# A selective-scan stage laid out with states on partitions, its input replicated by DMA, and the next batch prepared beside it

## The chip, the cores and the metric

The kernel runs on one core of one Trainium2 chip. The metric is the device time of an execution in microseconds; the comparison uses the median of several runs. A core has five engines with instruction queues of their own: TensorE (PE in the profile; PEld are its weight loads), VectorE (DVE), ScalarE (ACT), GpSimd (POOL) and SyncE (SP), which here issues most of the DMA transfers. Each queue is worked off in order.

## The reference

A block of four layers on x of 4 batches x 512 tokens x 512 channels, each added to x after a layernorm of it:

1. a gated MLP with int8-style smoothing and rounding (`smooth_quant`);
2. a feed-forward layer of inner width 1376 whose weights are looked up in a table of 16 values (`lut_weights`, `lut_ffn`);
3. a selective scan (a state-space layer) on the context input, gated by x;
4. a mixture of 32 experts with the 8 best for each token.

The change is about the third. Cut to what matters, for each batch, with 512 inner channels d, 16 states n and 512 time steps l:

```python
x = einsum('bld,ed->bel', hidden_states, in_proj_w)
x = silu(causal_conv4(x) + conv_b)                  # u
dt_low, Bm, Cm = split(einsum('bdl,ed->bel', x, x_proj_w))
dt = softplus(dt_proj_w @ dt_low + dt_proj_b)
A = -exp(A_log)
# over l, for every d and n:
state = state * exp(dt * A) + (dt * u) * B
y = sum_n state * C
y = (y + D * u) * silu(z)                           # z = layernorm(x)
```

## The kernel before, in words

The work is written as Python generators. A `yield` marks a step, `weave` takes steps from several generators in proportion to the step counts it is given, and a planner then orders the instructions by priority with costs of its own, within what data and buffers allow. The order of each engine's queue is therefore set when the kernel is built. `keep_in_program_order` fixes single DMAs in that order; `issue_after` (in the change) queues instructions directly behind a given one.

The stages are:

- **Smooth-quant and lookup** (L187 to L342). Four batches of `smooth_quant` are woven with the lookup of the feed-forward weights: one-hot rows on VectorE (L326) and matmuls with 32 weight columns on TensorE (L332). SP loads the index rows (L319), which GpSimd's own DMAs have laid out (L303).
- **Scan stage** (L988 to L1005). `lut_ffn` runs as one stream over all batches. A step (L366 to L381) has 16 matmuls of 256 columns, a tanh on ScalarE and two VectorE instructions. Woven with it, for each batch b, are `scan(b)`, and from b = 1 on `gate(b-1)` ahead of them and `route(b-1)` among them.
- **Experts** (L1006 to L1030): gathers (L811) and scatter-adds (L879) by indirect DMA on GpSimd, matmuls on TensorE. The first eight experts run beside the gate and the routing of the last batch. Then the two sums are added to x (L904 to L919).

`scan(b)` first prepares the batch. It loads the context cT (L428), and for each of four blocks of 128 channels it makes the projection pi (L433), its copy xin, the convolution (L440, L444) and u (L447, L448). Then it projects to dt, B and C (px, L454), and stores B and C in DRAM (xdbl, L457). The softplus follows (L465 to L476): Abs, Exp and Ln on ScalarE, the maximum (L470), a correction "lost" for small values (L472, L473) and two adds on VectorE. dt*u is one GpSimd product of 2048 columns (L477). The buffers u, dt, dtu and sz exist once, so a batch can't be prepared while the one before it is still scanned or gated.

Then come 64 units, each of one block e of channels and one state n. The 128 partitions are channels. For each n and each pair of blocks, `bc` brings one row of B and one of C to all partitions (L487: 512 KB, three buffers). A unit is: exp(dt*A) into a PSUM bank st (ScalarE, L490), dBu = dtu*B (GpSimd, L492), the scan along time (VectorE, L493), sc = st*C (VectorE, L495), and a matmul by the identity that adds sc into py[e] (TensorE, L496). An fp32 matmul appears as two records. After 16 states, L499 adds D*u.

`gate` multiplies by silu of the layernorm of x, transposes, and adds to x. `route` normalizes x, stores it to DRAM (L598, L599), makes the router's logits, the eight best, and 32 indirect scatters per batch into tables (L707). `layernorm` has two small VectorE instructions around a power on GpSimd (L102 to L105). `routing_constants` clears 16 tables and the two sums in DRAM from a zero tile (L580, L582), on SP's queue at the beginning of the scan stage.

Of the kernel before, what the change touches and what calls it, by code (L numbers as in the profile page):

```python
# [38 lines left out]
NST = 16  # L39
RANK = 16  # L40
# [18 lines left out]
class Kernel:  # L59
# [33 lines left out]
    def layernorm(self, dst, src, n):  # L93
# [8 lines left out]
        nc.vector.tensor_scalar(rs, mv[:, :, 1], LN_EPS, None, ALU.add)  # L102
        nc.gpsimd.tensor_tensor(rs, rs, self.mhalf[:, :n], ALU.pow)
        off = self.small.tile([P, n], F32, tag="ln_off", name="ln_off")
        nc.vector.scalar_tensor_tensor(off, mv[:, :, 0], -1.0, rs, ALU.mult, ALU.mult)  # L105
# [238 lines left out]
    def lut_ffn(self, bp, b):  # L344
# [4 lines left out]
        for hb in range(TPB // 2):  # L349
            xb = self.x[:, b * TPB + 2 * hb : b * TPB + 2 * hb + 2, :]  # L350
            xn = bp.tile([P, 2, HID], F32, tag="xn", name="xn", bufs=1)
            self.layernorm(xn, xb, 2)
            xT = bp.tile([P, KH, W], F32, tag="xT", name="xT", bufs=1)
            for k in range(0, KH, 2):
                pt = self.bank("t", "pt_x")
                for kk in range(2):
                    for i in range(2):
                        nc.tensor.transpose(
                            pt[:, kk * W + i * P : kk * W + (i + 1) * P],
                            xn[:, i, (k + kk) * P : (k + kk + 1) * P],  # L360
                            self.ident,
                        )
                nc.scalar.copy(xT[:, k : k + 2, :], pt.rearrange("p (k w) -> p k w", k=2))
# [35 lines left out]
    def scan_weights(self, mp):  # L399
# [15 lines left out]
        self.A = mp.tile([P, KH, NST], F32, name="A", bufs=1)  # L415
        nc.sync.dma_start(out=self.A, in_=t["A_log"])
        nc.scalar.activation(self.A, self.A, AF.Exp)
        nc.vector.tensor_scalar(self.A, self.A, -1.0, None, ALU.mult)
# [3 lines left out]
    def scan(self, mp, b):  # L422
# [3 lines left out]
        conv_b, dt_b, skip = (self.vecs[:, i, :] for i in range(3))  # L426
        cT = mp.tile([P, DC // P, S], F32, tag="sz", name="cT", bufs=1)
        nc.sync.dma_start(out=cT, in_=t["ctxT"][b].rearrange("(k p) l -> p k l", p=P))  # L428
        u = mp.tile([P, KH, S], F32, tag="u", name="u", bufs=1)
        for e in range(KH):  # L430
            pi = self.bank("d", "pi")
# [4 lines left out]
            xin = mp.tile([P, S + 3], F32, tag="dBu", name="xin", bufs=3)  # L436
            nc.gpsimd.memset(xin[:, :3], 0.0)
            nc.scalar.copy(xin[:, 3:], pi)
            acc = mp.tile([P, S], F32, tag="sc", name="acc", bufs=3)
# [3 lines left out]
            for j in (2, 1, 0):  # L443
                nc.vector.scalar_tensor_tensor(  # L444
                    acc, xin[:, j : j + S], self.conv_w[:, e, j : j + 1], acc, ALU.mult, ALU.add
                )
# [78 lines left out]
    def routing_constants(self, rp):  # L525
# [47 lines left out]
        for seen in self.seen:  # L573
            nc.vector.memset(seen, 0.0)
# [511 lines left out]
```

## Time and profile before

| | us |
|---|---|
| median of the three runs | 2109.53 (2107.18 to 2111.25) |
| profiled execution, its own time | 2106.76 |
| its span, first to last instruction | 2105.0 |
| smooth-quant and lookup | 0 to 322 |
| scan stage, to the end of its last scans | 322 to 1244 |
| experts | 1244 to 2063 |
| last sum | 2063 to 2105 |

Over the whole span TensorE is busy for 1825.7 us (87%), VectorE for 1240.6 (59%), GpSimd for 970.8 (46%) and ScalarE for 661.5 (31%). The mean granted clock of TensorE is 0.935. The numbers of one profiled execution are compared with one another; they differ from the median of the runs by some 3 us.

How to read the lines in this document: a line of a *group* gives the source line, engine, operation, output<-inputs, shapes and count, then the busy time in us and the mean length of one in ns, then how long the engine stood idle just before such instructions, and what ended those waits. A line of a *stretch* gives the window, its length, and the busy time of each engine in it (with instruction counts), the granted clock of TensorE, the share of the DMA engines that was busy, and GB/s. A line *in order of time* gives the start, the length, the engine and the instruction.

### The profile page before, as it was taken

Reading aid. Unit: us, or ns where it says so; the run is one execution under the profiler, and the core shown is the slowest. Engines: PE = TensorE matmul, PEld = TensorE weight load, DVE = VectorE, ACT = ScalarE, POOL = GpSimd, SP = SyncE. Lnnn points to the kernel's source line nnn. Section 1 sums busy time; section 2 is a strip of 40 time slices with the busy share of each in tenths; the row PEclk is TensorE's granted clock in tenths of the full one; section 3 lists DMA queues with packets and bytes.
Section 4 is the critical chain, followed back from the end, with each engine's and each line's share of the span. In section 5 each row is a group of like instructions: output and inputs, shape, how many; then the busy total and the mean of one; then the engine's idle time right before and its main releaser. Section 6 shows DMA issues by size and latency. Waiting matters only on the chain. (4 is left out here: it accounts for less than half of the span.)

```text
span 2105.0 us, 23555 instructions
## 1 busy us (share of the span) xinstructions
PE 1825.7 (87%) x8367; PEld 1072.7 (51%) x8377; DVE 1240.6 (59%) x2061; ACT 661.5 (31%) x1267; POOL 970.8 (46%) x836
## 2 busy tenths in 40 slices
PE   4777859988988998898979978859999999999980
PEld 2443427543554655464645535445656556656540
DVE  6788753599989878996799864213222223323232
ACT  1553451433433325332423232202222222222210
POOL 3111011166328742775158765655655555555531
PEclk9899979999989999899889989969999999999995
DMA  9421106144325422453225485657978887777655
GB/s 263 113 99 55 71 8 227 32 121 129 111 52 116 108 76 79 102 112 79 82 49 119 104 223 143 138 125 171 193 175 192 176 185 164 165 184 158 149 130 178
DMA packets 187699, 271.30 MB, mean 129 GB/s; under 512 B 43778, under 2 KB 90338, under 8 KB 187572
## 3 DMA queue, kind: packets, MB, share of 16 engines
q1 hardware_dynamic: 145828, 185.36, 31.3%
q0 software_dynamic: 41744, 84.34, 21.1%
q8 instruction: 68, 1.11, 0.2%
q14 instruction: 59, 0.48, 0.1%
HBM read 208.92 MB, written 69.18 MB: 132 GB/s over the span
## 5 line engine op out<-in xcount | busy, mean ns | idle before, releaser
L836 PE MATMUL pg<-exT,egu 128*128 128x320 f32 (+1 forms) x1536 | 404.4, 421 | 8.6 <-DVE eh L853 3.7
L492 POOL TENSOR_TENSOR dBu<-dtu,bc 128x512 f32<-128x512 f32 x256 | 322.6, 1274 | 149.5 <-DMA bc<-xdbl 108.8
L879 POOL DMA_INDIRECT sums<-ey,to x168 | 262.2, 1561 | 269.3 <-DMA sums<-ey,to 129.2
L836 PEld LDWEIGHTS pg<-exT,egu 128*128 128x128 f32 x1536 | 290.8, 192 | 127.5 <-issue 38.7
L493 DVE TENSOR_TENSOR_SCAN st<-st,dBu 128x512 f32<-128x512 f32 x256 | 308.0, 1221 | 57.9 <-ACT st L490 28.5
L496 PE MATMUL py<-sc,ident 128*128 128x512 f32 x512 | 267.1, 637 | 46.0 <-DVE sc L495 42.7
L490 ACT ACTIVATE st<-dt,A 128x512 f32<-128x512 f32 x256 | 170.7, 686 | 388.7 <-DVE sc L495 366.5
L811 POOL DMA_INDIRECT xg<-xln,tokens x168 | 163.6, 974 | 103.5 <-PE pt_g L824 40.8
L332 PE MATMUL pw<-oh,lut_t 128*32 128x344 bf16 (+1 forms) x2052 | 131.5, 376 | 70.7 <-DVE oh L326 70.7
L853 DVE SCALAR_TENSOR_TENSOR eh<-eh,pg 128x320 f32<-128x320 f32 (+5 forms) x144 | 61.1, 424 | 215.1 <-ACT eh L852 120.4
L371 PE MATMUL pgu<-xT,wg 128*128 128x256 f32 (+1 forms) x704 | 184.3, 400 | 1.3 <-DVE o L238 0.4
L865 PE MATMUL po_e<-ed,eh 128*128 128x512 f32 (+1 forms) x336 | 171.9, 631 | 11.3 <-ACT ey L878 3.9
L371 PE MATMUL pgu<-xT,wu 128*128 128x256 f32 (+1 forms) x704 | 179.8, 395 | 0.0
L496 PEld LDWEIGHTS py<-sc,ident 128*128 128x128 f32 x512 | 93.5, 197 | 162.0 <-DVE sc L495 106.6
L876 DVE TENSOR_SCALAR ey<-po_e,gates 128x512 f32<-128x512 f32 x64 | 45.8, 747 | 212.7 <-PE po_e L869 119.8
L495 DVE TENSOR_TENSOR sc<-st,bc 128x512 f32<-128x512 f32 x256 | 167.6, 679 | 5.2 <-PE py L496 0.5
L371 PEld LDWEIGHTS pgu<-xT,wg 128*128 128x128 f32 (+1 forms) x704 | 135.4, 197 | 60.7 <-issue 40.2
L387 PE MATMUL po_f<-wd,h 128*128 128x512 f32 (+1 forms) x352 | 164.3, 604 | 0.0
L878 ACT ACTIVATE ey<-po_e,gates 128x512 f32<-128x512 f32 (+1 forms) x104 | 68.8, 684 | 284.4 <-PE po_e L869 143.1
L371 PEld LDWEIGHTS pgu<-xT,wu 128*128 128x128 f32 (+1 forms) x704 | 138.2, 198 | 33.5 <-issue 12.3
L707 POOL DMA_INDIRECT table<-i_tok,to x128 | 127.1, 993 | 34.7 <-issue 23.2
L332 PEld LDWEIGHTS <-lut_t 128*32 128x32 bf16 x2052 | 59.8, 106 | 124.2 <-issue 84.4
(254 smaller groups left out, 2061.7 us busy)
## 6 DMA issues: line engine op xcount, KB each, us to landing
bc<-xdbl SPq DMA_DIRECT2D x128, 512.0 KB
egu<-in_w_gate SPq DMA_DIRECT2D x40, 384.0 KB
ix<-idx_b SPq DMA_DIRECT2D x16, 688.0 KB
egu<-in_w_up SPq DMA_DIRECT2D x40, 256.0 KB
ed<-in_w_down SPq DMA_DIRECT2D x40, 256.0 KB
ed<-in_w_down SPq DMA_DIRECT2D x80, 128.0 KB
sums<-zero SPq DMA_DIRECT2D x2, 4608.0 KB
acc<-sums SPq DMA_DIRECT2D x16, 512.0 KB
```

The costliest lines, as they stand in the source:

```text
L332: nc.tensor.matmul(pt[i][32 * c : 32 * c + 32, :step], lhsT=self.lut_t[:, j, g, :], rhs=oh[:, c * n + i * step : c * n + (i + 1) * step], ...
L371: nc.tensor.matmul(pg[:m, j * W : (j + 1) * W], lhsT=w[:, k, c * P : c * P + m], rhs=xT[:, k, :], start=k == 0, stop=k == KH - 1,)
L387: nc.tensor.matmul(po, lhsT=h[:m, c, i * P : (i + 1) * P], rhs=self.wd[:m, c, :], start=c == 0, stop=c == NIC - 1,)
L490: nc.scalar.activation(st, dt[:, e, :], AF.Exp, scale=self.A[:, e, n : n + 1])
L492: nc.gpsimd.tensor_tensor(dBu, dtu[:, e, :], bc[:, 0, :], ALU.mult)
L493: nc.vector.tensor_tensor_scan(st, st, dBu, 0.0, ALU.mult, ALU.add)
L495: nc.vector.tensor_tensor(sc, st, bc[:, 1, :], ALU.mult)
L496: nc.tensor.matmul(py[e], lhsT=self.ident, rhs=sc, start=n == 0, stop=n == NST - 1)
L811: nc.gpsimd.indirect_dma_start(out=xg[:m, :], out_offset=None, in_=xln, in_offset=bass.IndirectOffsetOnAxis(ap=tokens[:m, lo + j, col : co ...
L836: nc.tensor.matmul(pg[i][:, :hs], lhsT=w[:, k, i * P : (i + 1) * P], rhs=xT[:, k, z : z + hs], start=k == 0, stop=k == KH - 1,)
L865: nc.tensor.matmul(po[j][:m, :], lhsT=h[:, 0, b : b + m], rhs=wd[:, 0, :], start=True, stop=False)
L879: nc.gpsimd.indirect_dma_start(out=sums[j], out_offset=bass.IndirectOffsetOnAxis(ap=to[:m, lo + j, col : col + 1], axis=0), in_=y[:m, :], ...
```

## The change

- `scan(b)` is split into `prepare(b)` and `scan(b)`. `prepare(0)` is woven with six feed-forward steps; `prepare(b+1)` is a stream beside `scan(b)`. u has two buffers. The banks of PSUM are divided anew (t=2, m=2, y=1, d=3 for t=2, m=2, y=2, d=2).
- `prepare` computes the convolution from PSUM directly, with no copy xin. Softplus is done in blocks of 512 columns: the maximum becomes a Relu on ScalarE, and three of the VectorE instructions become GpSimd ones. dt and dt*u of each block go to DRAM (`dts`), by a DMA that GpSimd issues.
- A unit of the scan now has 16 states x 8 channels on the 128 partitions. Its dt and dt*u come by one DMA that replicates 8 rows 16 times (`d`: 512 KB a unit, four buffers); B and C for the whole batch stay in one tile BC. Of each four units, one has its product with C on GpSimd. Four units at a time are summed over states by four matmuls with 32 weight columns each, into the four quarters of py.
- `layernorm`'s two small VectorE instructions go to GpSimd; the feed-forward and the gate normalize one block at a time.
- `route` takes its weights from a mask instead of a product of one-hot rows, and the one-hot rows become bf16.
- The zeros for tables and sums (`scratch`) are written in the lookup stage, in 28 steps.

The diff, cut to its core:

```diff
     def layernorm(self, dst, src, n):
...
-        nc.vector.tensor_scalar(rs, mv[:, :, 1], LN_EPS, None, ALU.add)
+        nc.gpsimd.tensor_scalar(rs, mv[:, :, 1], LN_EPS, None, ALU.add)
         nc.gpsimd.tensor_tensor(rs, rs, self.mhalf[:, :n], ALU.pow)
...
-        nc.vector.scalar_tensor_tensor(off, mv[:, :, 0], -1.0, rs, ALU.mult, ALU.mult)
+        for i in range(n):
+            nc.gpsimd.tensor_scalar(off[:, i : i + 1], mv[:, i, 0:1], rs[:, i : i + 1], -1.0, ALU.mult, ALU.mult)
...
+    def prepare(self, mp, b):
...
+        u = self.u[b] = mp.tile([P, KH, S], F32, tag="u", name="u", bufs=2)
         for e in range(KH):
...
-            xin = mp.tile([P, S + 3], F32, tag="dBu", name="xin", bufs=3)
-            nc.gpsimd.memset(xin[:, :3], 0.0)
-            nc.scalar.copy(xin[:, 3:], pi)
-            acc = mp.tile([P, S], F32, tag="sc", name="acc", bufs=3)
+            acc = mp.tile([P, S], F32, tag="sc", name="acc", bufs=6)
...
             for j in (2, 1, 0):
+                a = 3 - j
                 nc.vector.scalar_tensor_tensor(
-                    acc, xin[:, j : j + S], self.conv_w[:, e, j : j + 1], acc, ALU.mult, ALU.add
+                    acc[:, a:], pi[:, : S - a], self.conv_w[:, e, j : j + 1], acc[:, a:], ALU.mult, ALU.add
                 )
...
-        nc.sync.dma_start(out=self.xdbl[b].rearrange("g n l -> (g n) l"), in_=xd)
+        nc.scalar.dma_start(out=self.xdbl[b].rearrange("g n l -> (g n) l"), in_=xd)
...
-            nc.scalar.activation(dtu[:, e, :], pd, AF.Abs, bias=dt_b[:, e : e + 1])
-            nc.vector.tensor_scalar(dt[:, e, :], pd, dt_b[:, e : e + 1], 0.0, ALU.add, ALU.max)
-        nc.scalar.activation(dtu, dtu, AF.Exp, scale=-1.0)
-        nc.vector.tensor_scalar(lost, dtu, 1.0, -1.0, ALU.add, ALU.add)
-        nc.vector.tensor_tensor(lost, dtu, lost, ALU.subtract)
-        nc.scalar.activation(dtu, dtu, AF.Ln, bias=1.0)
-        nc.vector.tensor_tensor(dtu, dtu, lost, ALU.add)
-        nc.vector.tensor_tensor(dt, dt, dtu, ALU.add)
-        nc.gpsimd.tensor_tensor(dtu, dt, u, ALU.mult)
+            d = mp.tile([P, 2, S], F32, tag="dt", name="dt", bufs=2)
+            dt, w = d[:, 0, :], d[:, 1, :]
+            nc.scalar.activation(w, pd, AF.Abs, bias=dt_b[:, e : e + 1])
+            nc.scalar.activation(dt, pd, AF.Relu, bias=dt_b[:, e : e + 1])
+            nc.scalar.activation(w, w, AF.Exp, scale=-1.0)
+            lost = mp.tile([P, S], F32, tag="sc", name="lost", bufs=6)
+            nc.vector.tensor_scalar(lost, w, 1.0, -1.0, ALU.add, ALU.add)
+            nc.gpsimd.tensor_tensor(lost, w, lost, ALU.subtract)
+            nc.scalar.activation(w, w, AF.Ln, bias=1.0)
+            nc.gpsimd.tensor_tensor(dt, dt, lost, ALU.add)
+            nc.gpsimd.tensor_tensor(dt, dt, w, ALU.add)
+            nc.gpsimd.tensor_tensor(w, dt, u[:, e, :], ALU.mult)
+            nc.gpsimd.dma_start(out=self.dts[b, e * P : (e + 1) * P], in_=d)
+            yield
+
+    def scan(self, mp, b):
...
+        BC = mp.tile([P, 2, S], F32, tag="BC", name="BC", bufs=1)
+        for g in range(2):
+            nc.sync.dma_start(
+                out=BC[:, g, :], in_=self.xdbl[b, 1 + g].unsqueeze(1).to_broadcast([NST, CPT, S])
+            )
+        for e in range(KH):
+            py = self.bank("y", f"py{e}")
+            for v in range(4):
+                scs = []
+                for j in range(4):
+                    r0 = e * P + 32 * j + CPT * v
+                    d = mp.tile([P, 2, S], F32, tag="d", name="d", bufs=4)
+                    nc.sync.dma_start(
+                        out=d, in_=self.dts[b, r0 : r0 + CPT].unsqueeze(0).to_broadcast([NST, CPT, 2, S])
+                    )
                     st = self.bank("d", "st")
-                    nc.scalar.activation(st, dt[:, e, :], AF.Exp, scale=self.A[:, e, n : n + 1])
+                    i = (e * 4 + v) * 4 + j
+                    nc.scalar.activation(st, d[:, 0, :], AF.Exp, scale=self.A[:, i : i + 1])
                     dBu = mp.tile([P, S], F32, tag="dBu", name="dBu", bufs=3)
-                    nc.gpsimd.tensor_tensor(dBu, dtu[:, e, :], bc[:, 0, :], ALU.mult)
-                    nc.vector.tensor_tensor_scan(st, st, dBu, 0.0, ALU.mult, ALU.add)
-                    sc = mp.tile([P, S], F32, tag="sc", name="sc", bufs=3)
-                    nc.vector.tensor_tensor(sc, st, bc[:, 1, :], ALU.mult)
-                    nc.tensor.matmul(py[e], lhsT=self.ident, rhs=sc, start=n == 0, stop=n == NST - 1)
+                    nc.gpsimd.tensor_tensor(dBu, d[:, 1, :], BC[:, 0, :], ALU.mult)
+                    sc = mp.tile([P, S], F32, tag="sc", name="sc", bufs=6)
+                    if j == 0:
+                        nc.vector.tensor_tensor_scan(sc, st, dBu, 0.0, ALU.mult, ALU.add)
+                        nc.gpsimd.tensor_tensor(sc, sc, BC[:, 1, :], ALU.mult)
+                    else:
+                        nc.vector.tensor_tensor_scan(st, st, dBu, 0.0, ALU.mult, ALU.add)
+                        nc.vector.tensor_tensor(sc, st, BC[:, 1, :], ALU.mult)
+                    scs.append(sc)
...
+                with ExitStack() as behind:
+                    for j in (3, 0, 1, 2):
+                        y = nc.tensor.matmul(
+                            py[32 * j : 32 * j + 32, :],
+                            lhsT=self.sum_states[:, v, :],
+                            rhs=scs[j],
+                            start=v == 0,
+                            stop=v == 3,
+                        )
+                        if j == 3:
+                            behind.enter_context(self.tc.issue_after(y.ins))
...
     def gate(self, mp, b):
...
         for e in range(KH):
+            sz = mp.tile([P, 1, S], F32, tag="sc", name="sz", bufs=6)
+            self.layernorm(sz, xb[:, e : e + 1, :], 1)
+            th = mp.tile([P, 1, S], F32, tag="sc", name="th", bufs=6)
...
     def clear(self, zero, tables, n):
...
         for s in self.sums:
+            for a in range(0, NT + 2, 3):
+                z = nc.sync.dma_start(
+                    out=s.rearrange("(a p) d -> p a d", p=P)[:, a : a + 3, :],
+                    in_=zero[:, :HID].unsqueeze(1).to_broadcast([P, 3, HID]),
+                )
+                self.tc.keep_in_program_order(z)
+                yield
...
     def route(self, rp, b):
...
-        ow = tl([P, TPB * TOPK, NE], F32, "ow")
-        nc.vector.tensor_tensor(
-            ow, oh, top.rearrange("p i k -> p (i k)").unsqueeze(2).to_broadcast([P, TPB * TOPK, NE]), ALU.mult
-        )
-        nc.vector.tensor_reduce(w, ow.rearrange("p (i k) e -> p i e k", i=TPB), AX.X, ALU.add)
+        mask = self.mask(rp, oh)
+        nc.vector.tensor_tensor(w, pr, mask, ALU.mult)
+        nc.vector.tensor_tensor(w, w, m.unsqueeze(2).to_broadcast([P, TPB, NE]), ALU.mult)
...
+                weave((islice(sq, 40), 40), (islice(lookups, 36), 36))
+                weave((sq, 30 * NB - 40), (lookups, 4 * len(k.jobs) - 36), (k.scratch(lc), 4 * CHAINS))
+            k.banks(early, t=2, m=2, y=1, d=3)
...
+            weave((k.prepare(mp, 0), preps), (islice(ffn_, 6), 6))
             k.routing_constants(rp)
...
             for b in range(NB):
-                n = steps + (4 if b == 0 else 0)
+                n = steps - (2 if b == 0 else 0)
                 streams = [(k.scan(mp, b), units), (islice(ffn_, n), n)]
+                if b + 1 < NB:
+                    streams.append((k.prepare(mp, b + 1), preps))
```

`sum_states`, which is new, holds ones where a partition's channel is that of the column, so that a matmul by it adds the 16 states of 8 channels. `A` is spread to the same layout by a small matmul at the start.

## The prediction

> **What bounds the kernel now.** I read the stretches first. They split the 2105.0 us span into smooth-quant and lookup (0 to 322 us), the scan stage (322 to 1244), experts, and a last sum. The change is almost wholly in the second, so I cut that at its scans (420 to 557, 645 to 780, 830 to 1000, 1070 to 1213) and at the gaps between, in which one batch is gated and the next prepared.
>
> ```profile
> core 0: us, PE busy (x) PEld busy (x) DVE busy (x) ACT busy (x) POOL busy (x), PEclk, DMA share, GB/s
> 322.00:420.00 98.00, 96.51 (x344) 64.48 (x344) 41.75 (x92) 29.55 (x47) 8.58 (x14) 0.97 0.40 139
> 420.00:557.00 137.00, 120.69 (x333) 58.38 (x334) 130.76 (x163) 51.64 (x79) 81.15 (x68) 0.98 0.41 111
> 557.00:645.00 88.00, 76.42 (x264) 44.78 (x263) 76.87 (x134) 34.55 (x56) 27.91 (x24) 0.90 0.30 87
> ...
> sum 922.00, PE 841.07 PEld 492.79 DVE 753.60 ACT 326.33 POOL 473.48; mean PE 93.45 PEld 54.75 DVE 83.73 ACT 36.26 POOL 52.61
> ```
>
> In a scan VectorE is full (130.76 of 137); before the first scan it has 41.75 of 98, and in a gap GpSimd stands still. No engine is full over the whole stage: VectorE's 753.6 of 922 is what a better overlap could squeeze. The groups name the work, and the instructions in order of time give the real pitch, since VectorE instructions overlap in the record.
>
> ```profile
> L492 POOL TENSOR_TENSOR dBu<-dtu,bc 128x512 f32<-128x512 f32 x256 | 322.6, 1274 | 149.5 <-DMA bc<-xdbl 108.8 <-DVE st L493 23.6 <-DVE x L394 5.6
> L493 DVE TENSOR_TENSOR_SCAN st<-st,dBu 128x512 f32<-128x512 f32 x256 | 308.0, 1221 | 57.9 <-ACT st L490 28.5 <-POOL dBu L492 26.7 <-issue 0.8
> L496 PE MATMUL py<-sc,ident 128*128 128x512 f32 x512 | 267.1, 637 | 46.0 <-DVE sc L495 42.7
> L490 ACT ACTIVATE st<-dt,A 128x512 f32<-128x512 f32 x256 | 170.7, 686 | 388.7 <-DVE sc L495 366.5
> L495 DVE TENSOR_TENSOR sc<-st,bc 128x512 f32<-128x512 f32 x256 | 167.6, 679 | 5.2 <-PE py L496 0.5
> ```
> ```profile
> 440.06 0.68 DVE L495 TENSOR_TENSOR sc<-st,bc 128x512 f32<-128x512 f32 x1
> 440.66 1.22 DVE L493 TENSOR_TENSOR_SCAN st<-st,dBu 128x512 f32<-128x512 f32 x1
> 441.79 0.41 DVE L381 SCALAR_TENSOR_TENSOR h<-g,pgu 128x256 f32<-128x256 f32 x1
> ```
>
> Pitch: product 0.60 us (440.66 - 440.06), scan 1.13. ScalarE waits 366.5 us for L495, so it is early. Two more views price what is new.
>
> ```profile
> 59.52 2.74 PE L332 MATMUL pw<-oh,lut_t 128*32 128x344 bf16 x49
> ```
> ```profile
> 610.66 4.50 POOL L477 TENSOR_TENSOR dtu<-dt,u 128x2048 f32<-128x2048 f32 x1 [29.45 <-DVE seen L684]
> ```
> ```profile
> 610.84 4.36 DVE L692 TENSOR_SCALAR over<-chosen 128x32 f32<-128x32 f32 x1
> 615.12 0.41 DVE L380 SCALAR_TENSOR_TENSOR g<-g,pgu 128x256 f32<-128x256 f32 x1
> 615.45 1.09 DVE L684 TENSOR_TENSOR seen<-seen,mask 128x32 bf16<-128x32 bf16 x1
> ```
>
> The first: 49 matmuls on 32 columns in 2.74 us, 56 ns each, though one alone is recorded at about 319 ns: column groups run side by side. The others: a tiny VectorE instruction lasts as long as the GpSimd product beside it.
>
> **What the Trainium skill says.** SBUF — State Buffer, section "Who interferes with whom": a VectorE instruction with two SBUF inputs, or in a two-port mode, and a GpSimd instruction that reads SBUF shut each other out for a whole instruction. L692 and L684 agree; the scan and C's product, with one operand in PSUM, keep their length beside GpSimd, as it also says. TensorEngine Tiling (Array Packing), "Key Properties": column tiles run independently, but a change of tiling mode drains the engine. The 56 ns agree with the first; no row isolates a drain. GPSIMD Engine Reference, "Performance versus the Vector engine": an add of 2048 takes 4497 ns on GpSimd against 2293 on VectorE; L477's 4505 and L476's 2291 agree, so work moved to GpSimd costs twice. DMA: Bandwidth & Descriptors, "Why a DMA increments its semaphore by 16 and not by 1": the engines used follow from both patterns' outer sizes; here 16 copies and 128 partitions, so all 16 (no run shows it yet).
>
> **Part by part, within the 922 us.**
>
> VectorE. A quarter of C's products leaves: 64 x 0.60 = -38.4. Softplus: 16 maxima to ScalarE at 0.67, -10.7; 12 instructions of 2048 columns (L473, L475, L476; pitch 2.2) to GpSimd, -26.4; L472 in quarters, 16 x 0.35 for 4 x 1.13, +1.1. Norm arithmetic: -5. The routing masks save some 2.6 per batch, three in the stage, -7.8. Sum: 753.6 - 87.2 = 666. Scans stay 256 x 1.13. Against that, with GpSimd nearly always busy, some 80 instructions that need the shared port (per batch 4 "lost", 4 u, 8 of the gate, a few of routing) wait. Bounds: none to a whole product, 0 to 100 us; I take half a product, 0.6 x 80 = 48. **714.**
>
> GpSimd. 473.5, plus 64 C products x 1.25 (pairs take 2.50) = 80; softplus 64 x 1.25 less L477's 18 = +62; 16 stores of dt and dt*u at 1.1 (L303's issues took that), +18; norms, two small instructions each for about 44 at 0.1 to 0.3 (a memset of three columns 0.10, iota 0.16), taken 0.2, and 16 more powers at 0.55, +27; the 0.30 gaps that L707's 96 scatters show, +29. **690.** Every product, store and norm is in one queue with dBu: what waits there holds up the next scan.
>
> TensorE, by pitch. A feed-forward half-matmul of 256 columns takes 0.216 us (8 in 1.73), one of 512 takes 0.43 (38 in 16.5). Feed-forward: 1408 x 0.216 + 352 x 0.43 + transposes 8 = 463; projections 128 x 0.43 = 55; gate and router (L518, L602, L607) about 33; scan 512 x 0.43 = 220: 771. The change still makes 256 scan matmuls, of 32 columns each, in 64 groups of four. Each is two records. Fully side by side a group takes 2 x 0.43 = 0.86, one after another 3.44; if both halves of a matmul must follow each other in the queue while the next column group overlaps, 5 x 0.43 = 2.15. I take 2.15, since the records alternate, and 0.2 per group for the drains (0 to 0.5): 64 x 2.35 = 150, so 702; at this stage's granted clock of 0.96, **731.** All serial it is 818, fully packed 646.
>
> DMA. A bc pair of 512 KB served two scans; now d, 512 KB, serves one: 256 loads for 128. In steady scan bc ran at 131 GB/s for a share of 0.49, so 267 GB/s when full and 1.96 us a load: +251 us of all engines. The stage's 0.41 x 922 = 378, less 35 for zeros moved, plus 251 and 8 for stores: 602 of some 785. Not the bound; cover is four buffers, some 10 us. SP's queue also carries route's stores, which can wait 20 us for w; three such waits cost up to 10 each beyond the cover. I take 0; both ends lie in the range.
>
> ScalarE gets Relu for a copy (+2) and up to 12 more pairs of table loads (2 x 1.28): 326 + 2 + 31 = 359, under half full. Taken 0: its 366 us of waiting covers it; uncovered, 2.6 per pair.
>
> Order. Preparing batch b+1 beside scan b removes what opens the gaps; u's second buffer and the trip through DRAM allow it. The batch's first scan waits for BC's two loads after the last product of the batch before (about 6 us), beside the gate's VectorE work: 0, or 18 in all uncovered. Zeros: 9.4 MB, 35 us of all DMA engines and 11.7 us that SP stands at cT (L428), go to the first stage, where DMA's share is 0.32. Their 30 issues pass SP's index loads, which already wait 136 us for L326: 0, or up to +8. The expert stage keeps its work; norms one block at a time there: 0, or +10.
>
> Sum. The longest engine is TensorE at 731, VectorE 17 behind. The scans ran at 95% of VectorE; for three engines so close I take the same loss, 731 / 0.95 = 770, plus 15 before the first batch is prepared: **785 instead of 922, -137.** The profiled execution took 2106.8 us around its span of 2105.0: 1970. The median shown is 2.7 above it: **1972.**
>
> **Rivals.**
> - Packing is full and the port waits vanish: VectorE at 666 / 0.95 + 15 = 716, -206: 1904. For it: L332. Against: fp32's two records and GpSimd at 690.
> - The column groups do not overlap in fp32 (the change does not do what it says for TensorE): 818 / 0.95 + 15 = 876, -46: 2064. For it: no fp32 packing is in this trace.
> - **Slower: the six sc buffers.** Four products are held until their group of matmuls has run, and prepare and the gate draw from the same six. With one spare, VectorE gets one unit (some 2.8 us) ahead while the group waits behind a feed-forward step (16 x 0.216 = 3.46) and runs 2.15: 2.8 us lost in each of 64 groups, 179, so 785 + 179 = 964, +42: 2152. It decides from 137 / 64 = 2.1 us a group. For it: before, each product frees its buffer alone. Against: matmuls can be queued between those of a step.
>
> **Chances.** Forecast 0.48, full packing 0.17, no overlap 0.23, sc buffers 0.12. The range, 1895 to 2075, takes in the first three with most of their unknowns. Within 0.2%, about what can be told from no change here, 0.02, from between the last two; slower 0.11; faster 0.87.
>
> **What would show it.** Right: no gaps without scans between batches; scan stage near 785 with TensorE, VectorE and GpSimd each near 90%; L692-like stretching of "lost" and u; groups of four py matmuls near 2.2 us; d's load never the longest wait. Wrong: VectorE's idle ahead of products or scans put down to PE py (sc buffers), to DMA d (loads), or to POOL dBu for over 60 us (GpSimd's queue is the bound); or a first stage longer than 330.

## The result, and the profile after

The changed kernel takes 2076.08 us (median of four runs, 2067.37 to 2081.98), the kernel before, on the same chip, 2108.36. The ratio is 0.985, with a 95% interval of 0.980 to 0.989: 32 us faster, where 137 were forecast and 2075 was the end of the range.

The profiled execution took 2081.98 us, span 2079.7. The last scans end at 1196 us, with the last D*u, 868 after the first stage. Before, the last D*u ended at 1242, 920 after the first stage (the table ahead has the rounder 1244 and 922; the forecast was 785). Of these 52 us, 6 are given back ahead, since the first stage ends at 328 us (322), and 13 behind: the first expert matmul starts 6 us after the last scans' end, at 1202, and started 7 ahead of it, at 1235. So 33 us remain there. From then on the changed kernel takes 878 us and the one before 870: 25 us are left of the profiled span.

The stretches below are the answer to those of before, cut where the work of the changed kernel changes: preparation of the first batch, its scan, and then for each later batch a stretch with the gate and the router's small work, and one with the 32 scatters (L806; L707 before) and the preparation of the batch after. The last stretch ends at the first expert matmul.

```profile
core 0: us, PE busy (x) PEld busy (x) DVE busy (x) ACT busy (x) POOL busy (x), PEclk, DMA share, GB/s
328.00:385.00 57.00, 46.31 (x155) 29.30 (x156) 24.70 (x76) 25.85 (x38) 19.65 (x29) 0.85 0.25 68
385.00:557.00 172.00, 146.23 (x548) 82.00 (x547) 135.01 (x180) 84.94 (x130) 133.59 (x118) 0.92 0.88 218
557.00:635.00 78.00, 62.94 (x270) 39.53 (x268) 68.72 (x129) 31.07 (x56) 43.01 (x52) 0.89 0.72 193
635.00:775.00 140.00, 113.67 (x413) 63.43 (x410) 98.18 (x130) 59.88 (x93) 127.77 (x117) 0.89 0.71 178
775.00:854.00 79.00, 62.65 (x273) 40.59 (x271) 70.43 (x130) 31.29 (x57) 42.77 (x52) 0.91 0.71 193
854.00:996.00 142.00, 115.75 (x415) 63.48 (x416) 97.40 (x133) 60.28 (x92) 127.73 (x117) 0.89 0.69 172
996.00:1068.00 72.00, 64.67 (x289) 42.82 (x288) 66.13 (x128) 28.95 (x53) 44.08 (x47) 0.93 0.78 213
1068.00:1184.00 116.00, 84.75 (x335) 47.81 (x333) 86.89 (x121) 35.61 (x60) 106.04 (x102) 0.90 0.85 205
1184.00:1202.00 18.00, 6.06 (x26) 3.42 (x27) 9.61 (x15) 7.32 (x18) 11.59 (x16) 0.50 0.85 217
sum 874.00, PE 703.02 PEld 412.38 DVE 657.06 ACT 365.19 POOL 656.25; mean PE 78.11 PEld 45.82 DVE 73.01 ACT 40.58 POOL 72.92
```

The sum is what the forecast was made for: VectorE and GpSimd are 75% busy, TensorE 80%. The lines above it say what this average hides. With the scatters GpSimd is all but full: 127.77 of 140, and 5.2 more go ahead of scatters, where it waits for nothing that the profile shows ("issue" in the next fence but one), 133 of 140; in the last such stretch it is 106.04 of 116. With the gate it has 43 of 78, and VectorE 68.72 of 78. In the first scan no engine is over 85%, and the loads take a share of 0.88. So what is fullest differs from one kind of stretch to the next.

The groups of the scan, over the whole execution:

```profile
L557 POOL TENSOR_TENSOR dBu<-d,BC 128x512 f32<-128x512 f32 x256 | 327.8, 1294 | 72.2 <-DVE st L563 36.3 <-DMA d<-dts 16.1 <-DVE seen L777 4.8
L563 DVE TENSOR_TENSOR_SCAN st<-st,dBu 128x512 f32<-128x512 f32 x192 | 231.3, 1218 | 87.2 <-POOL dBu L557 82.0 <-ACT st L555 5.0
L555 ACT ACTIVATE st<-d,A 128x512 f32<-128x512 f32 x256 | 174.1, 689 | 300.4 <-DVE sc L564 185.6 <-DMA d<-dts 72.4 <-DVE sc L560 37.6
L571 PE MATMUL py<-sc,sum_states 128*32 128x512 f32 x512 | 84.3, 690 | 68.1 <-DVE sc L564 68.1
L561 POOL TENSOR_TENSOR sc<-sc,BC 128x512 f32<-128x512 f32 x64 | 82.2, 1284 | 36.1 <-DVE sc L560 23.4 <-issue 6.0 <-DVE ln_mv L102 2.6
```

VectorE's scans now wait 82.0 us for GpSimd's dBu (26.7 before): the sign that the prediction had named for GpSimd's queue. What the queue holds in the stretch from 635 to 775 us is shown by GpSimd's groups there:

```profile
L557 POOL TENSOR_TENSOR dBu<-d,BC 128x512 f32<-128x512 f32 x44 | 55.3, 1274 | 1.4 <-DVE sc L560 0.6 <-DVE x L391 0.3
L806 POOL DMA_INDIRECT table<-i_tok,to x32 | 32.4, 1011 | 7.7 <-issue 5.2 <-DVE to L803 1.9 <-DMA d<-dts 0.3
L561 POOL TENSOR_TENSOR sc<-sc,BC 128x512 f32<-128x512 f32 x12 | 15.2, 1270 | 0.4 <-DVE sc L560 0.2
L524 POOL TENSOR_TENSOR lost<-dt,lost 128x512 f32<-128x512 f32 x4 | 5.1, 1266 | 2.2 <-DVE lost L523 2.2
L528 POOL TENSOR_TENSOR dt<-dt,u 128x512 f32<-128x512 f32 x4 | 5.1, 1264 | 0.2
```

L526 and L527 take the same again. Hardly anything here waits: the 12 products with C and 16 of the preparation, 36 us, all moved to this stretch or this engine by the change, stand in one queue with the dBu that VectorE wants.

Last, the price that the prediction knew least and the wait it had to guess, in order of time:

```profile
689.48 1.06 PE L571 MATMUL py<-sc,sum_states 128*32 128x512 f32 x8
...
693.45 1.11 DVE L523 TENSOR_SCALAR lost<-dt 128x512 f32<-128x512 f32 x1
...
707.79 2.08 DVE L523 TENSOR_SCALAR lost<-dt 128x512 f32<-128x512 f32 x1
```

This group of four matmuls, 8 records, takes 1.06 us, not 2.15 and not 3.44. Of the 59 groups that the trace shows in one piece, 47 take 1.06 or 1.07 us and 11 take 1.93 or 1.94. The Trainium skill, TensorEngine Tiling (Array Packing), "Key Properties", says that column tiles run independently; the trace shows it for fp32 too. And "lost", 0.43 us where GpSimd is idle (at 369 us), takes 1.11 beside a product and 2.08 beside a scatter and a product.

### The profile page after: what moved, and what is told of

Its sections match the earlier page's. It is cut to its first block, busy times and chain, and to the rows that moved or that the text cites. A ratio compares the mean times of both kernels' runs of the same rounds, so it can differ in the third digit from the quotient of the medians.

```text
span 2079.7 us, 24406 instructions
## 1 busy us (share of the span) xinstructions
PE 1702.7 (82%) x8377; PEld 1001.8 (48%) x8385; DVE 1140.4 (55%) x1946; ACT 700.6 (34%) x1327; POOL 1165.4 (56%) x1100
## 5 line engine op out<-in xcount | busy, mean ns | idle before, releaser
L557 POOL TENSOR_TENSOR dBu<-d,BC 128x512 f32<-128x512 f32 x256 | 327.8, 1294 | 72.2 <-DVE st L563 36.3
L563 DVE TENSOR_TENSOR_SCAN st<-st,dBu 128x512 f32<-128x512 f32 x192 | 231.3, 1218 | 87.2 <-POOL dBu L557 82.0
L555 ACT ACTIVATE st<-d,A 128x512 f32<-128x512 f32 x256 | 174.1, 689 | 300.4 <-DVE sc L564 185.6
L368 PE MATMUL pgu<-xT,wg 128*128 128x256 f32 (+1 forms) x704 | 191.3, 413 | 18.1 <-DVE h L378 18.0
L806 POOL DMA_INDIRECT table<-i_tok,to x128 | 128.0, 1000 | 33.6 <-issue 24.3
L571 PE MATMUL py<-sc,sum_states 128*32 128x512 f32 x512 | 84.3, 690 | 68.1 <-DVE sc L564 68.1
L564 DVE TENSOR_TENSOR sc<-st,BC 128x512 f32<-128x512 f32 x192 | 127.0, 676 | 1.1 <-PE py L571 0.6
L968 PE MATMUL po_e<-ed,eh 64*128 64x512 f32 (+1 forms) x336 | 114.9, 638 | 0.0
```

The source lines that it names most:

```text
L368: nc.tensor.matmul(pg[:m, j * W : (j + 1) * W], lhsT=w[:, k, c * P : c * P + m], rhs=xT[:, k, :], start=k == 0, stop=k == KH - 1,)
L555: nc.scalar.activation(st, d[:, 0, :], AF.Exp, scale=self.A[:, i : i + 1])
L557: nc.gpsimd.tensor_tensor(dBu, d[:, 1, :], BC[:, 0, :], ALU.mult)
L563: nc.vector.tensor_tensor_scan(st, st, dBu, 0.0, ALU.mult, ALU.add)
L564: nc.vector.tensor_tensor(sc, st, BC[:, 1, :], ALU.mult)
L806: scatter = nc.gpsimd.indirect_dma_start(out=tables[k % len(tables)], out_offset=bass.IndirectOffsetOnAxis(ap=to[:, i, k : k + 1], axis=0) ...
```

## The experiments

Two accounts of the missing 104 us (2076 less 1972) stood at first. **GpSimd's queue**: the work moved there is paid back in waits for dBu. **The loads**: d at a share near 0.9 paces the scan. A third, that TensorE or VectorE is short, is tried too. Ratios are to the kernel before on the same chip, with 95% intervals; the change itself has 0.985 (0.980 to 0.989) and, run again on another chip, 0.989 (0.986 to 0.992). So a difference of some 8 us between runs on different chips says nothing by itself. Where it helps, the length of the scan loop is given too, from the start of the first dBu to that of the last in the profiled execution: 815 us before, 799 in the change.

### What the packing gives

Each unit's product summed by a matmul of its own, not in groups of four:

```diff
-                    scs.append(sc)
...
-                    for j in (3, 0, 1, 2):
-                        y = nc.tensor.matmul(
...
+                    nc.tensor.matmul(
+                        py[32 * j : 32 * j + 32, :],
+                        lhsT=self.sum_states[:, v, :],
+                        rhs=sc,
+                        start=v == 0,
+                        stop=v == 3,
+                    )
+                    yield
```

> Undoes the grouping: each unit's product is summed by its own matmul at once, so sc buffers come free one by one and column groups no longer run side by side (0.86 us a unit for about 0.27). If the six sc buffers held by groups bound the stage, it falls by 20 us or more. If GpSimd bounds it, TensorE's 615 us become some 770 and the time rises by 0 to 40 us.

Ratio 1.020 (1.016 to 1.024), 2151 us. The stretch of its loop:

```profile
384.00:1270.00 886.00, 785.47 (x2559) 386.71 (x2559) 639.14 (x962) 340.24 (x553) 632.77 (x614) 0.95 0.72 181
```

TensorE is at 785 of 886. The groups are worth some 75 us, and without them the rest of the change is a loss of 2%.

The kernel before, with three of four scan matmuls left out (`if n % 4 == 3:`), so that y lacks three quarters of its states:

> The kernel before, leaving out three of four of the scan's matmuls (12 of 16 states are not summed into y): TensorE loses 192 x 0.86 = 165 us, no other engine loses work. If VectorE bounded the scans of the kernel before, as the prediction had it, the time stays within 10 us of 2110. If TensorE was the fullest engine there (771 us of work by pitch, 811 at the granted clock, in 913), it falls by 60 to 120 us, and the side-by-side column groups are what made the change faster.

Ratio 0.959 (0.956 to 0.962), 2016.5 us: 87 us of some 165 removed. So TensorE's work held the scans of before back, though only the first of them, where VectorE is fuller, had been shown in the forecast. The second scan of the kernel before and the gap after it:

```profile
615.00:772.00 157.00, 145.32 (x447) 84.30 (x447) 135.34 (x183) 50.91 (x85) 113.14 (x98) 0.95 0.43 97
772.00:838.00 66.00, 60.56 (x242) 38.94 (x242) 58.34 (x110) 31.11 (x49) 10.23 (x12) 0.97 0.26 84
```

and the loop of the run with few matmuls, in which VectorE has become the fullest, 688 of 740 us:

```profile
420.00:1160.00 740.00, 592.18 (x2010) 361.42 (x2009) 688.35 (x1039) 301.74 (x492) 465.85 (x406) 0.91 0.48 115
```

### Is TensorE, VectorE or the load short in the change?

Half the contraction of the feed-forward's gate and up matmuls left out (`for k in range(KH // 2)`):

> The changed kernel, leaving out half of the contraction of the feed-forward's gate and up products: TensorE loses 704 records of 0.216 us, 152 us, in the scan stage. If TensorE no longer bounds anything there, the time stays within 10 us of 2077. If the three engines hold one another up at some 80% each, taking work from any of them pays by a quarter to a half of it: 40 to 75 us.

One of two VectorE instructions of a feed-forward step (L377) and two of three taps of the convolution left out:

> The changed kernel, leaving out one of the two VectorE instructions of each feed-forward step and two of the three taps of the convolution: VectorE loses 88 x 0.33 + 32 x 0.66 = 50 us in the scan stage. If GpSimd alone bounds it, the time stays within 8 us of 2077. If the engines hold one another up, it falls by 12 to 30; if VectorE bounds it, by 40 to 50.

Loads of half the size: only dt comes, and dt*B stands in for dt*u*B:

```diff
-                        out=d, in_=self.dts[b, r0 : r0 + CPT].unsqueeze(0).to_broadcast([NST, CPT, 2, S])
+                        out=d[:, 0, :], in_=self.dts[b, r0 : r0 + CPT, 0, :].unsqueeze(0).to_broadcast([NST, CPT, S])
...
-                    nc.gpsimd.tensor_tensor(dBu, d[:, 1, :], BC[:, 0, :], ALU.mult)
+                    nc.gpsimd.tensor_tensor(dBu, d[:, 0, :], BC[:, 0, :], ALU.mult)
```

> Leaves out the dt*u half of every load of d (256 KB for 512) and multiplies dt by B in its place, so that no instruction of an engine goes away. If the loads bound the scan stage (DMA share 0.70 to 0.88 there, ScalarE waits 72 us for d), it falls by 50 us or more, to 2030 or less. If GpSimd's queue or the back and forth between engines bounds it, it stays within 15 us of 2077.

The same, with five buffers for dBu and eight for sc:

> As the run with half the load of d (dt times B in the place of dt*u times B), with the room this frees given to deeper buffers: five of dBu for three, eight of sc for six. Against that run, at 2076: if the engines lose time because they can run only few units ahead of one another, it falls by 20 to 60 us. If the order that the planner wrote into the queues is what makes them wait, or one engine's work is the bound, it stays within 10 us.

| left out | ratio | median, us |
|---|---|---|
| 152 us of TensorE | 0.978 (0.975 to 0.981) | 2056.1 |
| 50 us of VectorE | 0.981 (0.976 to 0.985) | 2063.0 |
| half of each load | 0.984 (0.982 to 0.986) | 2076.2 |
| half of each load, deeper buffers | 0.983 (0.980 to 0.987) | 2068.6 |

A tenth of TensorE's saving arrives, some 15 us, and at most a fifth of VectorE's: its 9 us are no more than the two runs of the change lie apart. Of TensorE's 152 us, reckoned by pitch at the full clock, only 96 show as less busy time: from 385 to 1190 us it is busy for 557 us instead of 653, with the granted clock at 0.82 instead of 0.90:

```profile
385.00:1190.00 805.00, 556.54 (x1911) 276.96 (x1912) 635.78 (x965) 337.77 (x554) 629.67 (x612) 0.82 0.77 198
```

The halved loads (DMA share 0.36 for 0.74 from 328 to 1202 us) and the buffers give nothing. So none of these alone is what the change lacks.

### GpSimd's share

All of C's products on VectorE:

```diff
-                    if j == 0:
-                        nc.vector.tensor_tensor_scan(sc, st, dBu, 0.0, ALU.mult, ALU.add)
-                        nc.gpsimd.tensor_tensor(sc, sc, BC[:, 1, :], ALU.mult)
-                    else:
-                        nc.vector.tensor_tensor_scan(st, st, dBu, 0.0, ALU.mult, ALU.add)
-                        nc.vector.tensor_tensor(sc, st, BC[:, 1, :], ALU.mult)
+                    nc.vector.tensor_tensor_scan(st, st, dBu, 0.0, ALU.mult, ALU.add)
+                    nc.vector.tensor_tensor(sc, st, BC[:, 1, :], ALU.mult)
```

> All of C's products on VectorE again: GpSimd loses 64 products (80 us), VectorE gains 64 x 0.60 = 38. If GpSimd's queue bounds the scan stage (680 us with its gaps, against 651 for VectorE), the stage falls by 40 to 80 us and the time to 2000 to 2040. If VectorE bounds it, the time rises by 20 to 38, to about 2100 to 2115. If the loads of d or the groups of matmuls bound it, it stays within 10 us of 2077.

The same, but GpSimd keeps its quarter in batch 0 and in the first half of the others, ahead of the scatters (`if j == 0 and (b == 0 or e < 2)`):

> GpSimd keeps its quarter of C's products in the first batch and in the first half of each later one, and gives it to VectorE in the second halves, where the scatters of the routing fall: 24 products, 30 us off GpSimd, 14 onto VectorE, in those stretches alone. If the load of GpSimd is uneven in time and its queue bounds only the stretches with scatters, this beats both the change and the version with all products on VectorE: 2045 to 2060 beside 2077 for the change. If only the sums of work count, it lies between the two, within 8 us of 2070.

Three of four scatters of the routing left out:

> Leaves out three of four scatters of the routing (24 of 32 for each batch), so that most slots of the tables stay empty. In the scan stage 72 GpSimd instructions of 1.0 us with 0.3 between them go away, 94 us. If GpSimd's queue is the bound in the stretches with scatters, the stage falls by 50 to 90 us. If the loads of d, VectorE or the groups of matmuls bound it, by less than 15.

Both, C on VectorE and few scatters:

> All of C's products on VectorE, and three of four scatters of the routing left out: GpSimd is down to some 510 us in the scan stage, VectorE at 688. If GpSimd's queue is what keeps the stage at 874, the gains of both add to 50 us or more, 2025 or less. If VectorE bounds as soon as GpSimd is relieved, this is no better than leaving out the scatters alone (2039), or slower.

The ratios: 0.980 (0.978 to 0.982) with C on VectorE, 0.980 (0.976 to 0.985) with the quarter kept early, 0.966 (0.964 to 0.969) with few scatters, 0.969 (0.966 to 0.972) with both. The first is some 10 us faster than the change, with VectorE given 38 us more to do; its interval overlaps the change's slightly, and lies clear of that of the change's second run below. The second, which was expected to beat both, is only as fast as the first. The stretches, of C on VectorE:

```profile
553.00:630.00 77.00, 64.23 (x274) 40.88 (x274) 69.74 (x130) 30.81 (x56) 35.84 (x42) 0.93 0.72 196
630.00:755.00 125.00, 105.26 (x375) 56.12 (x375) 100.52 (x138) 52.88 (x82) 108.20 (x102) 0.90 0.77 194
755.00:844.00 89.00, 73.54 (x314) 48.36 (x314) 74.90 (x139) 38.70 (x66) 43.50 (x50) 0.93 0.65 180
```

of few scatters:

```profile
554.00:630.00 76.00, 59.34 (x264) 37.06 (x262) 68.19 (x127) 30.42 (x54) 42.50 (x51) 0.93 0.72 198
630.00:735.00 105.00, 93.21 (x346) 51.64 (x347) 84.77 (x117) 50.51 (x78) 89.58 (x79) 0.95 0.84 205
735.00:833.00 98.00, 79.67 (x347) 51.47 (x349) 81.85 (x147) 41.57 (x72) 57.56 (x66) 0.91 0.72 191
```

and of both:

```profile
630.00:735.00 105.00, 95.20 (x352) 51.80 (x345) 95.08 (x132) 50.32 (x79) 80.08 (x76) 0.95 0.83 213
```

The first stretch with the scatters, from the first of them to the last, goes from 140 to 125 us for the same 44 units with C on VectorE, and to 105 us for 40 units with few scatters: 3.2, 2.8 and 2.6 us a unit. A part comes back in the stretches with the gate: from the second on they grow, and take feed-forward work and, with few scatters, some units with them (98 us for 79, TensorE 79.67 us for 62.65). So the gain of a whole batch is smaller: from the last dBu of the first batch to the last of the second it is 219 us in the change, 211 with C on VectorE, 201 with few scatters and 197 with both. With C on VectorE, GpSimd is still at 108.20 of 125, without what goes ahead of scatters, since the preparation's products are there. With few scatters it is at 85%, TensorE at 89 and VectorE at 81; giving VectorE the products too moves the load from 89.58 to 80.08 on GpSimd and from 84.77 to 95.08 on VectorE, and the stretch stays at 105. The loops take 776, 747 and 738 us: C's move gives 22 us by itself and 9 on top of few scatters, and in the whole time nothing is seen of the 9. So the gains don't simply add: once GpSimd isn't full, others are close behind.

The three sums of each softplus block (a subtraction and two additions) done by identity matmuls on TensorE and a ScalarE copy, alone and with C on VectorE, beside the change once more:

> A version that may beat the change: three of the four GpSimd instructions of softplus go to TensorE, which sums the four parts by identity matmuls in PSUM, and ScalarE copies the sum out. GpSimd loses 48 products of 1.27 (61 us), TensorE gains 64 x 0.86 = 55, ScalarE 11. At the shares measured so far (some 0.4 of what leaves GpSimd, 0.1 of what TensorE gains): -24 + 6, so about 2058. If the two sc buffers it holds in the place of one cost more, it rises.

> The same, with all of C's products on VectorE besides: GpSimd's queue falls by some 140 us, VectorE gains 31. If GpSimd's queue goes on paying, below the run before it, 2040 to 2055. If VectorE has taken its place as the fullest, equal to it or up to 10 slower.

> The changed kernel once more, on the same chip as the three others, so that they can be set against it: 2077, within 8 us.

Ratios 0.989 (0.985 to 0.992), 0.984 (0.981 to 0.987) and 0.989 (0.986 to 0.992), all on one chip. C's move gives some 10 us here too. The softplus on TensorE gives no gain by itself: GpSimd falls by 15 us in the first stretch with scatters, but TensorE rises to 122.83 of 138 there and to 164.60 of 177 in the first scan. That TensorE took over was not tried by itself.

The kernel before with a quarter of C's products on GpSimd, and nothing else (`if n % 4 == 0` in its scan):

> The kernel before with one part of the change alone: GpSimd does a quarter of C's products. VectorE's pitch of 0.60 us x 64 = 38 us leaves scans in which VectorE was busy for 130.76 of 137 us and GpSimd for 81. If a full VectorE bounds those scans, the time falls by 25 to 40 us from 2110. If GpSimd's queue holds up the scans as soon as it also carries products that wait for a scan, it falls by less than 10 or rises.

Ratio 1.024 (1.020 to 1.029), 51 us slower, though GpSimd was half idle there on average. Its waits (waiting instruction, what it waited for, us in total, times, longest), the first of which was 26.7 us before:

```profile
DVE st L498 <- POOL dBu L492: 77.9, 49, 5.2
...
PE py L500 <- POOL sc L496: 66.8, 44, 5.8
```

A product in GpSimd's queue holds up both its neighbours: the next dBu behind it and the matmul that needs it, here with three buffers of sc.

Layernorm's small instructions back on VectorE:

> Undoes one part: the two small instructions of each layernorm go back to VectorE. In the scan stage GpSimd loses some 90 instructions of 0.23 to 0.33 us, about 25 us, and its queue stands less in waits for other engines; VectorE gains about 8 us. If any work off GpSimd pays by some half of its length, the time falls by 8 to 20 us from 2077. If VectorE's small two-port instructions wait for GpSimd's long ones, it rises by 0 to 20.

Ratio 0.994 (0.991 to 0.997): some 19 us slower than the change. VectorE then waits for GpSimd's power, ahead of whatever stands behind it:

```profile
DVE ln_off L106 <- POOL ln_rs L104: 40.4, 25, 6.1
```

In the change this round trip costs VectorE 12.7 us, as a wait of L102 for L107. So this move to GpSimd pays. In the kernel before, which has the same order as this run, VectorE waited for the power for 2.8 us in the whole scan stage: the wait most likely came with the fuller queue of GpSimd.

### The overlap and the loads

u with one buffer, and batch b+1 prepared after batch b is gated, as before:

```diff
-        u = self.u[b] = mp.tile([P, KH, S], F32, tag="u", name="u", bufs=2)
+        u = self.u[b] = mp.tile([P, KH, S], F32, tag="u", name="u", bufs=1)
...
-                streams = [(k.scan(mp, b), units), (islice(ffn_, n), n)]
-                if b + 1 < NB:
-                    streams.append((k.prepare(mp, b + 1), preps))
+                streams = [(chain(k.prepare(mp, b), k.scan(mp, b)), preps + units), (islice(ffn_, n), n)]
```

> Undoes the preparation beside the scan: u has one buffer, and batch b is prepared after batch b-1 is gated, as before the change; all else is as in the change. If taking the gaps between batches out is what made the change faster, the time rises by 60 to 120 us, above the kernel before. If gain and loss lie elsewhere (the engines' queues are as full either way), by less than 30.

Ratio 0.997 (0.996 to 0.999): the overlap looks worth 26 us. But the first scan of this kernel, with nothing of the next batch's preparation beside it, shows something else (62 of its 64 units are in the first line):

```profile
377.00:522.00 145.00, 120.39 (x453) 70.56 (x452) 114.71 (x152) 57.81 (x92) 109.33 (x93) 0.91 0.96 235
529.00:592.00 63.00, 58.85 (x262) 40.12 (x261) 46.04 (x97) 34.28 (x57) 25.36 (x41) 0.98 0.31 101
592.00:752.00 160.00, 130.85 (x473) 73.07 (x472) 131.72 (x170) 60.61 (x96) 144.46 (x130) 0.87 0.86 212
```

The DMA share is 0.96 there, at 235 GB/s: one load of 512 KB in some 2.2 us. So the same order was run with loads of half the size, and that again with C on VectorE (both leave out the u of dt*u*B):

> The change with batch b+1 prepared after batch b is gated, as before (one buffer of u), and with loads of half the size: only dt is loaded and dt*B stands in for dt*u*B, so that part of the scan's input is left out. With whole loads and this order the ratio to before was 0.997, and there the first scan took 146 us for 64 units at a DMA share of 0.96 (2.27 us a unit). Theory 1, the loads bind a scan that has nothing beside it, and the overlap's worth is mostly that it hides them: the scan falls to 120 to 130 us for 64 units and the ratio to about 0.985, that of the change. Theory 2, the overlap itself is worth its 26 us: the units stay at 2.2 us and the ratio at about 0.997.

> As the other kernel of this call (prepared after the gate, half loads, so part of the scan's input left out), and with all of C's products on VectorE. A scan alone then has 64 x 1.73 = 111 us of VectorE and 82 us of GpSimd. If GpSimd's queue holds up a scan even with nothing of the preparation in it, this is 5 to 10 us faster than the other; if VectorE sets a bare scan, it is slower by up to 4 x 10 us.

With half loads: 0.982 (0.979 to 0.985), what the change has with half loads (0.984). So with loads out of the way, preparing beside the scan is worth nothing that these runs can tell. That the overlap's 26 us were the loads, which it spreads over more time, fits this ratio. The scans show it less clearly: from its first dBu to its last the first scan takes 141 us with half loads for 153 (120 to 130 had been expected), the two after it 159 and 161 for 160 and 162, and the last 163 for 168. With C on VectorE as well: 0.957 (0.954 to 0.960), 2018.5 us, the fastest variant of the change. The stretches show where. Half loads alone, where the second and third scans are the first and last line:

```profile
585.00:744.00 159.00, 125.98 (x464) 69.31 (x463) 131.09 (x170) 59.68 (x95) 143.91 (x130) 0.88 0.33 107
744.00:802.00 58.00, 51.43 (x223) 34.44 (x222) 41.32 (x87) 31.39 (x52) 23.75 (x39) 0.97 0.29 98
802.00:963.00 161.00, 126.13 (x464) 70.47 (x465) 131.64 (x175) 61.31 (x96) 145.31 (x130) 0.87 0.34 111
```

and with C on VectorE:

```profile
579.00:716.00 137.00, 113.60 (x441) 64.16 (x441) 131.93 (x180) 56.76 (x92) 123.72 (x113) 0.95 0.40 124
716.00:775.00 59.00, 54.86 (x246) 35.98 (x244) 44.01 (x93) 33.68 (x56) 23.57 (x39) 1.00 0.27 95
775.00:915.00 140.00, 116.12 (x437) 63.08 (x438) 133.49 (x185) 57.09 (x91) 126.14 (x115) 0.90 0.41 128
```

A scan with scatters beside it takes 160 us with GpSimd at 143.91 of 159, 91% without what goes ahead of scatters, and 137 to 140 us without C's quarter, VectorE at 96%. The quarter costs 57 us here and 10 in the change, where the preparation's products fill the same stretch of GpSimd anyway. The order of the change with both half loads and C on VectorE was not tried.

## Why the prediction was wrong

Step by step, as the forecast had them:

- **GpSimd, 690: right.** 656 busy, and 16 more ahead of scatters, 672. **DMA, 602 of 785: right as a share** (0.77 forecast, 0.74 measured from 328 to 1202 us), though a load costs some 2.2 us, not 1.96. **The six buffers of sc** cost nothing (deeper ones give nothing, and C's products wait 0.6 us for py). **Zeros**: the first stage ends 6 us later, inside the 8.
- **TensorE, 731: too high.** The group takes 1.06 us instead of 2.35: the mechanism of the rival "packing is full". 463 + 55 + 33 + 64 x 1.06 = 619 by pitch, 688 at the granted clock of 0.90, where 0.96 was assumed. That is the prediction's "fully packed 646" at a lower clock.
- **VectorE, 714: too high.** 657, while the forecast without port waits was 666. The waits exist (L523 takes 0.84 us in the mean for 0.43 alone) and are small: 16 x 0.41 = 7 us for L523; the others that the forecast counted were not measured one by one.
- **The step that failed is "for three engines so close I take the same loss, 731 / 0.95 = 770, plus 15".** All three terms came in at or below their sizes, and the stage still took 868: 688 / (868 - 15) = 0.81, not 0.95. By luck the oversized terms hid a part of this: with the measured 688 the same step would have given 688 / 0.95 + 15 = 739. Taking one efficiency over the whole stage supposes that the engines are wanted evenly. They aren't: the routing's 32 scatters, 38 us of GpSimd, fall into one stretch of each batch. With 44 dBu, 12 products with C and 16 of the preparation there, GpSimd needs 133 us, and the stretch took 140. The three stretches with scatters make 398 us, the three with the gate 229, where GpSimd is 57% busy and VectorE 90%; the first scan 172, its preparation 57, the tail to the first expert matmul 18: 874. That GpSimd is the bound with the scatters is shown by its full stretch, by the runs that leave scatters or C's quarter out of it, and by the run with half loads and C on VectorE. It is a part of the miss: with few scatters the loop is 52 us shorter, where the stage was 83 us over its forecast. Another 6 us of the miss lie ahead of the stage, and some 22 behind it, where the forecast took 0, or 10.
- **"Preparing batch b+1 beside scan b removes what opens the gaps": the gaps shrank, the time hardly did.** From the start of a batch's last dBu to that of the next one's first, 10 to 12 us are left, in which BC is loaded and the gate begins (forecast: 0, or 6 each). Before, such a gap of 66 to 72 us was full of TensorE's work (60.56 of the 66 from 772 to 838 us), and a scan with scatters took 157 to 164. From the first dBu to the last it was 815 us, and it is 799 now. GpSimd "stands still" in a gap, but what was moved out of it, 16 products of the preparation, went into the stretch where GpSimd has no room. The larger part of the gain, 41 us, is a shorter first preparation (57 us for 98), from which feed-forward work was moved into the loop (TensorE 46 us for 97). That the groups made the room for it there is likely, but no run shows it by itself.
- **"In a scan VectorE is full (130.76 of 137)"** was read from the first scan alone. In the later ones TensorE is fuller, 145 of 157, and taking its matmuls away gave 87 us. The change removes just that bound, and this is what it gains by: some 75 us by the run without groups, of which 43 are lost again in the rest of the change.

What stays open: the first scan of the change, 172 us, has no full engine, and halving the loads shortens it by some 8 us without a gain at the end; what sets the stretches with the gate, where VectorE is the fullest but taking 50 us from it gave at most 9; how much the order that the planner wrote into the queues adds, which no run changes by itself; and why softplus on TensorE brings nothing. Of the versions that compute all of the reference, the two with all or part of C's quarter on VectorE are the fastest here: 0.980, some 10 us ahead of the change.

## What to carry to other kernels

Cut a stage where its mix of work changes, and sum each engine's work for each stretch before and after the change; work that moves to an engine which is half idle on average is only free if it lands where that engine is idle. A queue that feeds every unit of a loop (dBu here) makes all else on the same engine costly: price what is moved there by the waits of those that need the feed. And undo parts together as well as one by one: half loads and C's quarter on VectorE gave 0 and 10 us alone, and some 32 and 57 where the next batch was not prepared beside the scan.

## What the runs showed of the hardware

- Four fp32 matmuls of 128 x 32 weights on four column groups take 1.06 us in most groups. No pause is visible at the change from full-width matmuls: the group starts at 689.48, where the last one of the feed-forward ends at 689.55 (687.66 + 1.89; the profiler models these ends). The matmul behind it starts 1.00 us after the group does, so the change back can cost at most 0.14 us beyond the 0.86 of two records by pitch, an estimate.
- A load that replicates 32 KB sixteen times into 512 KB, in runs of 4 KB, takes some 2.2 us at a DMA share of 0.96, 235 GB/s. At that share all 16 engines take part, as the prediction had it.
- In three kernels TensorE's granted clock was lower where it was less busy: 0.95 over the loop without groups (TensorE busy for 89%), 0.90 in the change (81%, 385 to 1190 us), 0.82 with half of the feed-forward's contraction left out (69%). It is no strict rule: before, from 1000 to 1070 us, the clock is 0.91 with TensorE busy for 96%. With a lower clock, part of what a TensorE saving promises doesn't arrive (96 us of 152 did, in busy time). Why the clock falls was not tried.
- A VectorE instruction of 512 fp32 columns (L523) takes 0.43 us alone and 0.84 in the mean of 16, up to 2.08 beside GpSimd's work.
